# When stores are issued on a shared DMA queue: moving stores behind the operations that make them, and one kind of load to another queue

## The chip, the core and the metric

The kernel runs on one core of a Trainium2 chip. The core has engines that each run their own list of instructions in order: TensorE (PE in the profile; its weight loads are PEld), VectorE (DVE), ScalarE (ACT), GpSimd (POOL) and SyncE (SP), which here only issues DMAs. A DMA is issued from the list of one of these engines, and if the data that it reads or the buffer that it writes isn't ready, the engine's list stands at that instruction until it is. The metric is the time of the kernel on the device in microseconds (us).

## What is computed

The input `x` has the shape (4, 1024, 256), in float32. Two layers follow each other, both with a residual:

```python
x = x + attn(layernorm(x), w_attn, w_proj)
x = x + ffn(layernorm(x), ...)
```

`attn` is causal self-attention with 16 heads of 16 values over the 1024 positions of each of the 4 sequences, with a bias that falls off with distance by a slope for each head:

```python
att = einsum('bhqd,bhkd->bhqk', q, k) / sqrt(D) + where(rel <= 0, slopes * rel, -inf)
y = einsum('bhqk,bhkd->bhqd', softmax(att), v)
return y.transpose(0, 2, 1, 3).reshape(B, T, C) @ w_proj.T
```

`ffn` first attends over the 4 sequences at each position, which is a small attention of 4 by 4 for each position and head, then normalises, and then chooses an expert: each row of 256 values goes through one of 8 two-layer networks with a GELU, the one with the larger number among its two best. Its output is added and normalised again:

```python
h = layernorm(x + attn_out)
_, top_i = top_k(softmax(h @ router_w.T + router_b), 2)
assign = max(top_i, axis=-1)                  # one expert for each row
out[row] = gelu(h[row] @ w1[e].T + b1[e]) @ w2[e].T + b2[e]   # e = assign[row]
return layernorm(h + out)
```

## The kernel before, in words

The work is one long program in `fast_layer`, with the order of the instructions fixed by the kernel itself: the framework adds the semaphores, and doesn't reorder.

**Attention.** The rows are cut into 16 batches `n`, each of 256 positions (`W`) of one sequence: `batches[n] = (c, b)`, where `c` is the block of positions and `b` the sequence, with `c` running outside. The attention of a batch is a unit `u`; for the last block (`c` = 3) each batch is two units of 128 positions, so there are 20 units. The 16 heads are taken in 4 groups `g` of four. In a unit, each group takes one to three *rounds* of scores; a round is PE's `score` (line 955: 16 small products `sk` or more, two `exp` on ACT that write `p`, and a mask on POOL, line 986), and later PE's `weigh` (line 992), which multiplies the probabilities `p` with the values `v` into `pv`.

Two rounds are a *place* `p` of the main loop (lines 2242 to 2254); there are 80 places. Each place has two times at which other work is put between the scores: `E_slot(2p)` and `E_slot(2p + 1)`, half places, for elementwise work and for DMAs that are due, and `D_slot(p)` for products on PE. What goes where comes from two tables, `of_E` and `of_D`, filled at lines 2104 to 2120, from lists of work with due times, `due_E` and `due_D` (line 2129), and from a planner that keeps its own estimate of the time on PE, DVE and ACT (`time`) and starts the steps of the second layer when their inputs should be there.

**What goes through DRAM.** Three things are written to DRAM by one unit and read by others.

- *Keys and queries.* `project_qk` (line 879) makes half of the heads' queries and keys, copies them from PSUM to `kq` on DVE and stores them to `k_of[b]` (line 895 for `c` = 0, line 899 after). `fill_slots` (line 925) loads the keys of all positions so far and the queries, laid out with 32 rows for each head, into `slots` (line 939): four DMAs for each group and unit, issued when the unit before has done its last round of that group.
- *Values.* `value` (line 901) makes a batch's values, copied by ACT into `values[b % 2]`, and stores them to `v_of[b]` (line 916). `load_values` (line 918) loads the values of all earlier blocks of the sequence into `values[b % 2]` (line 923), since the two buffers are shared by the four sequences. It is put at `E_slot(2q + 1)`, where place `q` is the first of the unit before.
- *Outputs.* After a group pair's last round, `weigh` stores `yt` to `y_of[u]` (line 1036). Row 16 of each head's 32 holds the sum of its probabilities. `load_sums` (line 1043) reads the sums back (line 1045), `invert` (line 1049) takes the reciprocal on DVE and stores it to `r_of[u]` (line 1053), `load_y` (line 1057) loads the reciprocals spread over 16 rows into `su` (line 1068) and the outputs into `yc` (line 1071), `divide` multiplies the two on DVE, and `project` multiplies with `w_proj` on PE and adds to `x`. In the planner's time these steps are due 7, 14, 18, 29 and 31 us after the unit's last `weigh` (line 76).

For `c` = 0 the stores of `y` and `v` are issued by ACT. All other DMAs named here are issued by SP, in the order of the program.

**The second layer.** `front` (line 1551) is a generator with a step for each piece of work on one block of 128 positions of all four sequences: it normalises into `u`, projects, attends over the sequences, adds, normalises again and picks the expert. Two DMAs store the rows for the experts: `x` plus a bias, in four parts (line 1569, from `for_later`), and `u` (line 1768). Most fronts run inside the attention; at most two at a time (`start_fronts`). The buffers of `x` are ten; `load_next` loads a later batch's `x` when `left_x` says that both fronts of an earlier block have stored theirs. The last front and the experts, which gather their rows with indirect DMAs on POOL (line 1813) and scatter the results (line 1929), come after the attention, in the loops from line 2356 on.

Of the kernel before, what the change touches and what calls it, by code (L numbers as in the profile page):

```python
# [47 lines left out]
PC = W // P  # L48
# [557 lines left out]
def fast_layer(ctx: ExitStack, tc: tile.TileContext, odd, x, wq, wk, wv, wp, w_in, w_out, w_r,  # L606
# [244 lines left out]
    wqk = const("wqk", [P, 2, CC, C], into=pad)  # L851
    held = {}

    def x_norm(n, stage):
        c, b = batches[n]
        src = lambda i: xs[c, b][:, i]
        if stage == 0:
            held["norm", n] = norm_stats(src, PC, f"x_{n}", "_x")
        elif stage == 1:
            norm_root(held["norm", n][1], PC)  # L860
        else:
            xn = act.tile([P, PC, C], F32, tag="xn", name=f"xn_{n}")
            norm_apply(lambda i: xn[:, i], src, PC, *held.pop(("norm", n)), f"x_{n}")
            held["xn", n] = xn
# [14 lines left out]
    def project_qk(n, half):  # L879

        c, b = batches[n]
        xt = held["xt", n]
        pm = bank(f"qkp_{n}_{half}")
        for k in range(2):
            for cc in range(CC):
                nc.tensor.matmul(
                    pm[:, k * W:(k + 1) * W], wqk[:, k, cc, half * P:(half + 1) * P],
                    xt[:, cc], start=cc == 0, stop=cc == CC - 1,
                )
        kq = act.tile([P, 2, W], F32, tag=f"kq{half}", name=f"kq_{n}_{half}", bufs=KQ_BUFS)  # L890
        nc.vector.tensor_copy(kq.rearrange("p k w -> p (k w)"), pm)
        rows_ = slice(half * P, (half + 1) * P)
        if c == 0:
            held["kq", n, half] = kq
            nc.sync.dma_start(k_of[b][rows_, :2 * W], kq.rearrange("p k w -> p (k w)"))
        else:
            own = k_of[b][rows_, :W]
            both = bass.AP(own.tensor, own.offset, [own.ap[0], ((c + 1) * W, 2), (1, W)])
            nc.sync.dma_start(both, kq)

    def value(n):
        c, b = batches[n]
        xt, vt = held.pop(("xt", n)), values[b % 2]
        pm = bank(f"vp_{n}")
        for i in range(PC):
            for cc in range(CC):
                nc.tensor.matmul(
                    pm[:, i * C:(i + 1) * C], xt[:, cc, i * P:(i + 1) * P], wv_sb[:, cc],
                    start=cc == 0, stop=cc == CC - 1,
                )  # L910
        own = vt[:, PC * c:PC * (c + 1)]
        nc.scalar.copy(
            own[:, :, 0:H * VD].rearrange("p n (h d) -> p n h d", d=VD)[:, :, :, 0:D],
            pm.rearrange("p (n h d) -> p n h d", n=PC, d=D),
        )
        (nc.sync if c else nc.scalar).dma_start(v_of[b][:, PC * c:PC * (c + 1)], own)

    def load_values(u):
        n, i, _ = units[u]
        c, b = batches[n]  # L920
        known = NT if i else PC * c
        if known:
            nc.sync.dma_start(values[b % 2][:, :known], v_of[b][:, :known])

    def fill_slots(u, g):

        n, i, _ = units[u]
        c, b = batches[n]
        if b == 0 and c and i == 0:
            query_rows(c, g)  # L930
        for j in range(4):
            at, row_ = slice(j * S, j * S + D), (4 * g + j) * D
            n_cols = W + (c + 1) * W
            src = k_of[b][row_:row_ + D, :n_cols]
            if c == 0:
                row_ = (4 * (g % 2) + j) * D
                src = held["kq", n, g // 2][row_:row_ + D].rearrange("p k w -> p (k w)")
            queue = nc.scalar if u == 0 and j % 2 else nc.sync
            queue.dma_start(slots[g][at, :n_cols], src)
# [52 lines left out]
    def weigh(rounds_):  # L992
# [29 lines left out]
        for k, ((u, g), of_part) in enumerate(parts):  # L1022
            n, i, size = units[u]
            c = batches[n][0]
            pv = pm[:, k * W:k * W + size * P]
            if of_part[0][0] == 0 and g % 2 == 0:
                held["yt", g // 2] = ends.tile(
                    [P, 2, W], F32, tag="yt", name=f"yt_{u}_{g}", bufs=2
                )
            yt = held["yt", g // 2][:, :, :size * P]  # L1030
            if of_part[0][0] == 0:
                nc.scalar.copy(yt[:, g % 2], pv)
            else:
                nc.vector.tensor_tensor(yt[:, g % 2], yt[:, g % 2], pv, ALU.add)
            if g % 2 and of_part[-1][0] == n_rounds(u) - 1:
                (nc.sync if c else nc.scalar).dma_start(
                    y_of[u][g - 1:g + 1].rearrange("g p w -> p g w"), yt
                )

    def heads_of(n):  # L1040
        return y_of[n].rearrange("g p w -> (g p) w").rearrange("(h s) w -> h s w", s=S)

    def load_sums(u):
        part_of_row = units[u][2] * H
        nc.sync.dma_start(
            sums[u], heads_of(u)[:, D].rearrange("h (k w) -> h k w", w=part_of_row)
        )
# [503 lines left out]
    def front(i, fact, more, last):  # L1551
# [14 lines left out]
        def for_later(t):  # L1566

            nc.vector.tensor_tensor(at_x(t), at_x(t), row(B2), ALU.add)
            nc.sync.dma_start(rows_of[:, t, C:2 * C], at_x(t))

        def flipped(src, name):
            dst = fact.tile(
# [16 lines left out]
        yield "E", 1.7  # L1589
        for t in range(B):  # L1590
            for_later(t)
        left_x[i // PC] += 1
        yield "DQ" if more else "D", 2.8
        qkv = fact.tile([P, B, 3 * C + E], F32, tag="qkv", name=f"qkv_{i}")

# [169 lines left out]
        yield "E", 2.2  # L1765
        nc.vector.tensor_tensor(u, u, wide(row(G1)), ALU.mult)
        nc.vector.tensor_tensor(u, u, wide(row(B1)), ALU.add)
        nc.sync.dma_start(rows_of[:, :, 0:C], u)
        yield ("DC" if last else "D"), 0.8

        if last:
# [270 lines left out]
        return end  # L2042

    def start_fronts():
        while queue and len(running) < 2:
            running.append(Running(queue.pop(0)))

# [56 lines left out]
    for u, (n, i, size) in enumerate(units):  # L2104
        c, b = batches[n]

        q = begins[u - 1] if u else -2
        e = begins[u + 1]
        if u == n:
            if n > 2:  # L2110
                at_E(2 * begins[n - 3], lambda n=n: to_load.append(n))
            for k in range(3):
                at_E(2 * q - 7 + k, lambda n=n, k=k: x_norm(n, k), (1.0, 0.0, 0.8)[k])
            at_D(q - 2, 0.9, lambda n=n: turn(n))

            at_D(q - (n == 0), 1.7, lambda n=n: project_qk(n, 0))
            at_D(q + (n > 0), 1.7, lambda n=n: project_qk(n, 1))
            at_D(q + 2, 1.7, lambda n=n: value(n))
        if u > 1:
            at_E(2 * q + 1, lambda u=u: load_values(u))  # L2120


    due_E, due_D = [], []
# [67 lines left out]
    def E_slot(k, some=True):  # L2191
        for cost, what in of_E.pop(k, []) + pop_due(due_E, time["PE"]):
            what()
            busy("DVE", cost)
        load_next()
        if tables and fetching:
            experts.fetch()
# [44 lines left out]
    for p in range(len(rounds) // 2):  # L2242
# [10 lines left out]
        fill()  # L2253
        E_slot(2 * p + 1, then)
    weigh_next(waiting)
    attention.close()
    half_of.clear()
    tail_banks.append(ctx.enter_context(pool("ps_m", 3, space=PSUM)))
# [72 lines left out]
    def take(it, at):  # L2331
# [4 lines left out]
        for cost in it.more:  # L2336
            free["PE"] = max(free["PE"], at) + cost
        it.next()
        it.ready = end + LAG
        if on == "PE" and it.kind != "d":  # L2340
            it.ready = end + COPIED
# [34 lines left out]
    n = 0  # L2376
# [98 lines left out]
```

## Time and profile before

| | |
|---|---|
| median of 3 runs | 839.2 us |
| lowest, highest | 836.48, 842.09 us |
| the profiled execution | 839.28 us, its span 837.1 us |
| mean clock granted to PE | 0.940 |

The span runs from the first to the last instruction, and some 2 us lie around it. All durations below come from this one execution. Lines of the profile name an engine, the line of the kernel, an operation and what it writes and reads (`out<-in`). Nearly all instructions of PE, DVE and ACT are recorded through one helper at line 587, so they are told apart by what they write; DMAs have their own line. `SPq` is SP's list, in which a DMA's time is that of its issue and not of the transfer. The page's last part counts the DMAs, with the size of each:

```profile
slots<-k SPq DMA_DIRECT2D x128, 80.0 KB
k<-kq SPq DMA_DIRECT2D x32, 256.0 KB
v<-v SPq DMA_DIRECT2D x16, 288.0 KB
v<-v SPq DMA_DIRECT2D x4, 1152.0 KB
x<-in_x_dram SPq DMA_DIRECT2D x16, 256.0 KB
y<-yt SPq DMA_DIRECT2D x16, 256.0 KB
rows<-x SPq DMA_DIRECT2D x32, 128.0 KB
slots<-k SPq DMA_DIRECT2D x64, 64.0 KB
rows<-u SPq DMA_DIRECT2D x8, 512.0 KB
```

The 16 `v` DMAs of 288 KB are 12 stores and 4 loads; the loads of later blocks have 576, 864 and 1152 KB, four each. SP's list carries 79.63 MB on its queue (q1), ACT's 4.25 MB (q10).

### The profile page before, as it was taken

The page shows a single profiled execution, that of the slowest core. Times are in us where ns is not written, and L with a number is a line of the kernel's source. Part 1 is how long each engine was busy: PE and PEld are TensorE (multiplying, and loading weights), DVE is VectorE, ACT ScalarE, POOL GpSimd, SP SyncE. Part 2 cuts the span into 40 slices and gives each one's busy share as a digit, 9 for nine tenths or more (in the row PEclk, how much of TensorE's full clock was granted, in tenths as well). Part 3 has the DMA queues.
Part 4 walks back from the last instruction along what each step waited for, and adds up shares of the span by engine and source line. Part 5 has one row for each costly group of instructions (what it writes and reads, how often), then busy time and mean ns, then how long its engine had stood idle before and what let it go on. Part 6 is the DMA issues. An engine that isn't in the chain of part 4 may idle for free. (4 is left out here: it accounts for less than half of the span.)

```text
span 837.1 us, 22503 instructions
## 1 busy us (share of the span) xinstructions
PE 719.4 (86%) x8917; PEld 540.2 (65%) x8917; DVE 544.6 (65%) x1316; ACT 416.6 (50%) x625; POOL 251.1 (30%) x360
## 2 busy tenths in 40 slices
PE   4988879995999999998989999999983689678982
PEld 2766657674666756665667767787762368567772
DVE  7337224546678877946964739487695869884663
ACT  1455436563647556735654658578460235323540
POOL 5534102211113221102211212122130235637885
PEclk9799889998999999998999999999997699978997
DMA  7454444424344324333354635445315512333430
GB/s 215 117 148 137 143 134 134 144 63 123 94 119 129 108 77 147 98 104 95 93 142 141 185 109 144 123 126 158 94 53 195 177 37 90 93 97 120 124 103 24
DMA packets 75219, 99.56 MB, mean 119 GB/s; under 512 B 19496, under 2 KB 58723, under 8 KB 74596
## 3 DMA queue, kind: packets, MB, share of 16 engines
q1 hardware_dynamic: 64576, 79.63, 32.1%
q0 software_dynamic: 4864, 14.16, 5.6%
q10 hardware_dynamic: 5668, 4.25, 1.7%
q8 instruction: 73, 1.20, 0.6%
q14 instruction: 38, 0.31, 0.1%
HBM read 61.55 MB, written 35.12 MB: 115 GB/s over the span
## 5 line engine op out<-in xcount | busy, mean ns | idle before, releaser
L587 ACT ACTIVATE p<-sk 128x1024 f32<-128x1024 f32 (+1 forms) x320 | 287.0, 939 | 162.8 <-PE sk L587 147.8
L986 POOL TENSOR_SCALAR_AFFINE_SELECT p<-p 128x512 f32<-128x512 f32 (+1 forms) x160 | 103.6, 651 | 397.8 <-ACT p L587 395.9
L587 PE MATMUL sk<-slots 32*128 32x128 f32 (+1 forms) x3456 | 181.7, 328 | 21.2 <-DVE kq L587 10.0
L587 PEld LDWEIGHTS sk<-slots 32*128 32x128 f32 x3456 | 138.1, 188 | 64.9 <-issue 26.8
L587 PE MATMUL pv<-p,v 128*32 128x128 f32 (+1 forms) x3456 | 144.5, 314 | 10.4 <-ACT p L587 4.6
L587 PEld LDWEIGHTS pv<-p,v 128*32 128x32 f32 x3456 | 96.7, 111 | 48.3 <-issue 8.3
L587 PE MATMUL qkvp<-w_in,ut 128*128 128x264 f32 (+1 forms) x224 | 79.1, 489 | 0.0
L587 PEld LDWEIGHTS qkvp<-w_in,ut 128*128 128x128 f32 x224 | 40.3, 194 | 26.7 <-issue 22.4
L587 PE MATMUL oe<-w,ge 128*128 (+1 forms) x152 | 45.2, 423 | 12.9 <-DVE given L587 4.5
L587 PE MATMUL qkp<-xt,wqk 128*128 128x256 f32 x208 | 54.4, 407 | 0.2 <-ACT p L587 0.2
L1813 POOL DMA_INDIRECT given<-rows,rows x38 | 43.2, 1137 | 27.6 <-DVE at_t L587 11.6
L587 PE MATMUL hid<-mt,w 128*128 128x128 f32 x304 | 47.0, 293 | 0.5 <-ACT ge L587 0.5
L587 PEld LDWEIGHTS qkp<-xt,wqk 128*128 128x128 f32 x208 | 39.6, 200 | 11.1 <-issue 3.3
L587 ACT COPY qkv<-qkvp 128x512 f32<-128x512 f32 (+1 forms) x28 | 15.3, 555 | 58.5 <-PE qkvp L587 43.9
L587 PEld LDWEIGHTS hid<-mt,w 128*128 128x128 f32 x304 | 41.9, 200 | 2.0 <-ACT ge L587 1.0
L587 DVE COPY qkv<-qkvp 128x264 f32<-128x264 f32 x28 | 11.9, 431 | 46.9 <-PE qkvp L587 46.8
L1929 POOL DMA_INDIRECT out_dram<-o,out_rows x38 | 38.9, 1024 | 8.8 <-issue 6.3
L587 DVE TENSOR_REDUCE sc<-pr 128x64 f32<-128x1024 f32 x32 | 39.0, 1220 | 1.1
L587 PEld LDWEIGHTS oe<-w,ge 128*128 128x128 f32 x152 | 28.0, 205 | 17.8 <-DVE given L587 5.7
L587 DVE TENSOR_TENSOR pv<-qkv,sc 128x1024 f32<-128x1024 f32 x32 | 39.2, 1224 | 0.4 <-issue 0.3
L587 DVE TENSOR_TENSOR pr<-qkv 128x1024 f32<-128x1024 f32 x32 | 39.2, 1226 | 0.0
L587 PE MATMUL vp<-wv,xt 128*128 128x256 f32 x128 | 35.3, 423 | 0.0
(333 smaller groups left out, 1040.2 us busy)
## 6 DMA issues: line engine op xcount, KB each, us to landing
slots<-k SPq DMA_DIRECT2D x128, 80.0 KB
k<-kq SPq DMA_DIRECT2D x32, 256.0 KB
v<-v SPq DMA_DIRECT2D x16, 288.0 KB
v<-v SPq DMA_DIRECT2D x4, 1152.0 KB
x<-in_x_dram SPq DMA_DIRECT2D x16, 256.0 KB
y<-yt SPq DMA_DIRECT2D x16, 256.0 KB
rows<-x SPq DMA_DIRECT2D x32, 128.0 KB
slots<-k SPq DMA_DIRECT2D x64, 64.0 KB
```

What stands on the lines that cost most here:

```text
L587: ins = made(*args, **kwargs)
L986: nc.gpsimd.affine_select(blocks, blocks, pattern=[[0, 2], [0, size], [1, P]], compare_op=ALU.is_ge, fill=0.0, base=0, channel_multiplier=-1,)
L1813: nc.gpsimd.indirect_dma_start(out=self.hx, out_offset=None, in_=t.rows_of, in_offset=bass.IndirectOffsetOnAxis(ap=t.rows_[:, self.j:self. ...
L1929: ins = nc.gpsimd.indirect_dma_start(out=out.rearrange("t n c -> (t n) c"), out_offset=bass.IndirectOffsetOnAxis(ap=t.table.out_rows[:, t. ...
```

## The change

A list `stores` takes the place of issuing at once: a store is put on it with a key and an age, and is issued at the next `E_slot` that finds it with an age of one, or just before a load that reads what it writes. The stores of `k` and `v` for `c` > 0, of `y` for `c` > 0, and of `x` and `u` go this way. The age is raised at each `E_slot`, after the stores of age one have gone and before the front's steps of that slot, so that a store from a `weigh` goes half a place later, one from a `D_slot` between half a place and a place, and one from a front's elementwise step a whole place later. `start_fronts` issues waiting stores of `u` before it starts a front. In the loop after the attention, all stores on the list go right after the step that made them.

`load_values` is issued from ACT's list and not from SP's, and half a place later. The first half of `project_qk` comes one place earlier for `c` > 0. The stores of `x` of one front go together, after all four additions, and `left_x` is raised when they are issued.

```diff
@@ -851,6 +851,19 @@
     wqk = const("wqk", [P, 2, CC, C], into=pad)
     held = {}
 
+
+
+    stores = []
+
+    def store(key, what):
+        stores.append([key, 0, what])
+
+    def issue_stores(*keys, age=None):
+        due = [it for it in stores if it[0] in keys or age is not None and it[1] >= age]
+        for it in due:
+            stores.remove(it)
+            it[2]()
+
     def x_norm(n, stage):
         c, b = batches[n]
         src = lambda i: xs[c, b][:, i]
@@ -896,7 +909,7 @@
         else:
             own = k_of[b][rows_, :W]
             both = bass.AP(own.tensor, own.offset, [own.ap[0], ((c + 1) * W, 2), (1, W)])
-            nc.sync.dma_start(both, kq)
+            store(("k", n, half), lambda: nc.sync.dma_start(both, kq))
 
     def value(n):
         c, b = batches[n]
@@ -913,14 +926,19 @@
             own[:, :, 0:H * VD].rearrange("p n (h d) -> p n h d", d=VD)[:, :, :, 0:D],
             pm.rearrange("p (n h d) -> p n h d", n=PC, d=D),
         )
-        (nc.sync if c else nc.scalar).dma_start(v_of[b][:, PC * c:PC * (c + 1)], own)
+        to = v_of[b][:, PC * c:PC * (c + 1)]
+        if c:
+            store(("v", b), lambda: nc.sync.dma_start(to, own))
+        else:
+            nc.scalar.dma_start(to, own)
 
     def load_values(u):
         n, i, _ = units[u]
         c, b = batches[n]
         known = NT if i else PC * c
         if known:
-            nc.sync.dma_start(values[b % 2][:, :known], v_of[b][:, :known])
+            issue_stores(("v", b))
+            nc.scalar.dma_start(values[b % 2][:, :known], v_of[b][:, :known])
 
     def fill_slots(u, g):
 
@@ -931,6 +949,7 @@
         for j in range(4):
             at, row_ = slice(j * S, j * S + D), (4 * g + j) * D
             n_cols = W + (c + 1) * W
+            issue_stores(("k", n, g // 2))
             src = k_of[b][row_:row_ + D, :n_cols]
             if c == 0:
                 row_ = (4 * (g % 2) + j) * D
@@ -1033,15 +1052,18 @@
             else:
                 nc.vector.tensor_tensor(yt[:, g % 2], yt[:, g % 2], pv, ALU.add)
             if g % 2 and of_part[-1][0] == n_rounds(u) - 1:
-                (nc.sync if c else nc.scalar).dma_start(
-                    y_of[u][g - 1:g + 1].rearrange("g p w -> p g w"), yt
-                )
+                to = y_of[u][g - 1:g + 1].rearrange("g p w -> p g w")
+                if c:
+                    store(("y", u), lambda to=to, yt=yt: nc.sync.dma_start(to, yt))
+                else:
+                    nc.scalar.dma_start(to, yt)
 
     def heads_of(n):
         return y_of[n].rearrange("g p w -> (g p) w").rearrange("(h s) w -> h s w", s=S)
 
     def load_sums(u):
         part_of_row = units[u][2] * H
+        issue_stores(("y", u))
         nc.sync.dma_start(
             sums[u], heads_of(u)[:, D].rearrange("h (k w) -> h k w", w=part_of_row)
         )
@@ -1566,7 +1588,11 @@
         def for_later(t):
 
             nc.vector.tensor_tensor(at_x(t), at_x(t), row(B2), ALU.add)
-            nc.sync.dma_start(rows_of[:, t, C:2 * C], at_x(t))
+
+        def store_later():
+            for t in range(B):
+                nc.sync.dma_start(rows_of[:, t, C:2 * C], at_x(t))
+            left_x[i // PC] += 1
 
         def flipped(src, name):
             dst = fact.tile(
@@ -1589,7 +1615,7 @@
         yield "E", 1.7
         for t in range(B):
             for_later(t)
-        left_x[i // PC] += 1
+        store(("x", i), store_later)
         yield "DQ" if more else "D", 2.8
         qkv = fact.tile([P, B, 3 * C + E], F32, tag="qkv", name=f"qkv_{i}")
 
@@ -1765,7 +1791,7 @@
         yield "E", 2.2
         nc.vector.tensor_tensor(u, u, wide(row(G1)), ALU.mult)
         nc.vector.tensor_tensor(u, u, wide(row(B1)), ALU.add)
-        nc.sync.dma_start(rows_of[:, :, 0:C], u)
+        store(("u", i), lambda: nc.sync.dma_start(rows_of[:, :, 0:C], u))
         yield ("DC" if last else "D"), 0.8
 
         if last:
@@ -2042,6 +2068,8 @@
         return end
 
     def start_fronts():
+        if queue and len(running) < 2:
+            issue_stores(*[it[0] for it in stores if it[0][0] == "u"])
         while queue and len(running) < 2:
             running.append(Running(queue.pop(0)))
 
@@ -2113,11 +2141,11 @@
                 at_E(2 * q - 7 + k, lambda n=n, k=k: x_norm(n, k), (1.0, 0.0, 0.8)[k])
             at_D(q - 2, 0.9, lambda n=n: turn(n))
 
-            at_D(q - (n == 0), 1.7, lambda n=n: project_qk(n, 0))
+            at_D(q - (n == 0 or c > 0), 1.7, lambda n=n: project_qk(n, 0))
             at_D(q + (n > 0), 1.7, lambda n=n: project_qk(n, 1))
             at_D(q + 2, 1.7, lambda n=n: value(n))
         if u > 1:
-            at_E(2 * q + 1, lambda u=u: load_values(u))
+            at_E(2 * q + 2, lambda u=u: load_values(u))
 
 
     due_E, due_D = [], []
@@ -2192,6 +2220,9 @@
         for cost, what in of_E.pop(k, []) + pop_due(due_E, time["PE"]):
             what()
             busy("DVE", cost)
+        issue_stores(age=1)
+        for it in stores:
+            it[1] += 1
         load_next()
         if tables and fetching:
             experts.fetch()
@@ -2253,6 +2284,7 @@
         fill()
         E_slot(2 * p + 1, then)
     weigh_next(waiting)
+    issue_stores(age=0)
     attention.close()
     half_of.clear()
     tail_banks.append(ctx.enter_context(pool("ps_m", 3, space=PSUM)))
@@ -2336,6 +2368,7 @@
         for cost in it.more:
             free["PE"] = max(free["PE"], at) + cost
         it.next()
+        issue_stores(age=0)
         it.ready = end + LAG
         if on == "PE" and it.kind != "d":
             it.ready = end + COPIED
```

## The prediction

> **What bounds the kernel now.** I read the engines' busy shares first, then the table of stretches, then who waited for whom, and last the order of time around the largest hole.
>
> ```profile
> PE 719.4 (86%) x8917; PEld 540.2 (65%) x8917; DVE 544.6 (65%) x1316; ACT 416.6 (50%) x625; POOL 251.1 (30%) x360
> ```
>
> TensorE (PE) is the fullest engine. In the stretches of 20 us its busy time shows where it isn't full. The columns are PE, PEld, DVE, ACT and POOL busy, the granted clock, the DMA share and GB/s:
>
> ```profile
> 80.00:100.00 20.00, 16.06 (x113) 12.08 (x114) 6.90 (x20) 7.16 (x10) 2.11 (x4) 0.83 0.44 124
> 100.00:120.00 20.00, 14.77 (x145) 11.14 (x147) 3.88 (x13) 5.68 (x8) 1.28 (x2) 0.83 0.51 144
> ...
> 180.00:200.00 20.00, 11.23 (x184) 7.65 (x176) 11.27 (x13) 9.32 (x13) 3.85 (x6) 0.92 0.23 61
> ...
> 380.00:400.00 20.00, 16.75 (x203) 9.94 (x202) 16.55 (x41) 10.72 (x14) 3.28 (x5) 0.83 0.39 114
> ...
> 420.00:440.00 20.00, 16.21 (x336) 13.55 (x339) 11.43 (x20) 11.52 (x17) 3.56 (x6) 0.91 0.48 140
> ```
>
> Over 40 to 620 us, the attention, PE stands idle 41.7 us (20 minus its busy time, summed over 29 stretches). These five hold 25.0 of it. In them VectorE (DVE) is not full either: it stands too. The waits over the whole span (total, times, longest) say for what:
>
> ```profile
> DVE inverse L587 <- DMA sums<-y: 40.9, 8, 11.0
> ...
> DVE yc L587 <- DMA yc<-y: 28.2, 7, 8.6
> ...
> PE sk L587 <- DVE kq L587: 10.0, 3, 8.5
> ...
> PE op L587 <- DVE yc L587: 5.8, 1, 5.8
> ```
>
> So DVE stands 69.1 us for transfers, and PE then for DVE. Both transfers are issued by SyncE's queue (SP). Its own waits between 40 and 640 us:
>
> ```profile
> SPq L1036 <- ACT yt L587: 72.2, 20, 8.3
> ...
> SPq L1068 <- DMA r<-inverse: 22.9, 10, 5.3
> ...
> SPq L916 <- ACT v L587: 19.3, 8, 5.0
> SPq L899 <- DVE kq L587: 18.9, 7, 5.0
> ...
> SPq L939 <- DMA k<-kq: 14.6, 7, 3.0
> ```
>
> SP stands mostly in front of stores whose data isn't made yet. With the rows for other releasers: y stores (L1036) 100.4, k stores (L899) 28.0, v stores (L916) 19.3, u stores (L1768) 14.2, x stores (L1569) 9.0 us, 171 in all, and 14.6 for k to land before slots are read back. The worst hole in order of time:
>
> ```profile
> 182.81 0.38 SPq L1036 DMA_DIRECT2D y<-yt  x1
> 182.88 0.34 DVE L587 RECIPROCAL inverse<-sums 128x32 f32<-128x32 f32 x1
> ...
> 183.28 1.80 SPq L939 DMA_DIRECT2D slots<-k  x4
> ...
> 185.18 0.37 SPq L1053 DMA_DIRECT2D r<-inverse  x1
> ...
> 194.15 0.69 DVE L587 TENSOR_TENSOR yc<-yc,su 128x512 f32<-128x512 f32 x1 [8.59 <-DMA yc<-y]
> ...
> 200.27 2.19 PE L587 MATMUL sk<-slots 32*128 32x256 f32 x16 [8.53 <-DVE kq L587]
> ```
>
> The y store held SP until 182.81; the inverse, ready at 183.2, was stored at 185.18 only, behind four slot loads; DVE stood until 194.15, and PE until 200.27 for the kq copy queued behind. From about 640 us on, fronts and experts end in a chain on POOL (L1813, L1929).
>
> **What the Trainium skill says.** "DMA: Bandwidth & Descriptors", Anatomy of one DMA, says that a DMA's semaphore wait is served on the issuing sequencer before dispatch, and that most of a fixed cost of about 2 us is the receipt of the written bytes. The trace agrees: L1036 stands on SP, and r, issued at 185.18, lets su go at 186.84. Its Queues, rings and completion order gives SP and ACT a ring each on the same 16 DMA engines, served in turn; so a large load on ACT's ring lets a small one on SP's pass, where on one ring it goes ahead. No run yet shows that gain. "TensorE: Matmul & The Clock Gate", HAM oscillation, says that idle gaps over about 3.4 us throttle PE. It fits: the 16 score matmuls after the 8.53 us gap took 2.19 us, against 0.94 to 1.15 elsewhere, and the five stretches have clocks of 0.83 to 0.92.
>
> **The change part by part.** What is at stake: 25.0 us of holes and the 5.8 us at 630 us (op waiting for yc), 31 together. The lower clock in these stretches and the one after the third (0.91), one minus clock times PE busy, is 12 us more: 43 at most, 0.62 us for each of the 69.1 us that DVE stands.
>
> *y, k and v stores later.* No DMA is added; 32 y, 24 k and 12 v stores go to the next or next but one half place (about 4 us each: 80 places in some 600 us). By then the slot loads, which pace SP, have had their PE wait and the store's data is mostly there. What was queued behind a y store (3.1 us each, 100.4/32), above all slots, sums, r, su and yc, moves up. I go through the holes. At 82 to 92, SP stood about 3 us for k to land before eight slot loads; sums came last, at 88.55: half 0 of qk is now projected a place earlier, so I take 3 us off DVE's stall and 2 off PE's. At 102 to 113 sums was issued at 108.12 behind a v store, a 3 us wait for k and a 288 KB values load: 5 us off the 5.2 that PE stood and its start-up. At 185 to 194: r at 183.3 in place of 185.18, 2 us. At 391 to 397: r and yc earlier by one y wait, 1 us. At 426 to 432: sums came behind a y store and slot loads, 2 us. At 630: y stood 0.5 us between r and su: 0.5. Sum 12.5 us of 31; the same share of 12 is 5 us of clock. Bounds: 0 if all waits merely change name, 43 if all go.
>
> *What the delay adds.* A k store of half 1 is forced just before the slot load that needs it, where a group has two rounds (8 units): landing costs SP up to 3.0 us each, as the k row shows, 24 us of SP at most; the slots are needed four places later, so I take 1 us on PE. Queued behind are r, su and yc, and DVE waits for those. A y store forced by its sums would do likewise, but a unit's sums come 5.7 to 18 us behind its own last y store (276.02 to 281.68, 469.96 to 487.94): 0. Buffers: yt is written again two places on, u with the next but one front, x loads come after x stores (353.21, then 355.11) but have places to spare; 0 each, up to 4 us (a 512 KB u store before DVE may write) if that cover goes.
>
> *Values on ACT.* Sixteen loads of 288 to 1152 KB leave SP: 16 x 0.37 us of issue, and their bytes leave its ring. They cost ScalarE the same 6 us, where it is 50 to 65% busy between exps. Its wait, for PE's weighing of the unit before last, is over by then, since the exp ahead of it needs a later PE product. I take 1 us on PE; bounds 0 and 6, plus any wait. The gain by the ring isn't seen in this trace; 0 to 3 us for each of eight sums stalls, I take 1 us over all.
>
> *x and u stores, tail.* 32 and 8 stores; SP stood 23 us for them in the attention, and little hung on it: 1 us. In the tail stores go out at once after each step; the four x stores come after four adds instead of between. 0, within 1 us either way. The planner's slots shift with the moved projection; which front steps fit changes: plus or minus 5 us.
>
> Sum: 12.5 + 5 - 1 - 1 + 1 + 1 = 17.5 us off; I take off 3.5 for stalls that come back at the next wait, r's landing (22.9 us on SP, untouched): 14. The profiled execution took 839.28 us, its span 837.1; 825.3. The median, 839.2, is the same; I forecast **825 us**.
>
> **The rivals.** *First: new waits swallow it.* Every sums and yc still needs store, landing, load, landing, and DVE has as little between inverse and divide as before (two operations at 183). If DVE's stalls fall by only 5 of 69 us, 5 x 0.62 gives 836. For it: r's 22.9 us and the 3.4 to 5.2 us that sums take to land. Against: stores stand for 171 us. *Second, slower: stores now land in front of their own readers.* If a forced k or y store stands ahead of the sums chain in most of the 16 units past the first four, at 3.0 us each, DVE stands 48 us longer less the gain of 23 (14/0.62): 25 x 0.62 is 15 us, 855. It decides from where forced landings outlast the 23 us, eight of them. Against: the gaps of 5.7 us and more between y and its sums. A projection moved onto a busy place would add to it. *Third: the stores aren't later in fact.* Stores asked for by a reader at once keep the old order; then only the values move, 837.
>
> **How the numbers follow.** Forecast 0.62 (its own range 812 to 831), first and third rival together 0.24 (831 to 846), second 0.14 (846 to 862). 8 times in 10: 808, where 31 of the 43 us have gone, to 846, where part of the second's case is left out. One per cent, 8.4 us, is about what can be told from no change. Faster 0.62, same 0.24, slower 0.14.
>
> **What would show it.** Right: L1036 on SP falls under 40 us; DVE for sums and yc falls from 69 to about 45; PE fills 80 to 120 and 180 to 200, clock 0.95 or more. Values loads stand on ACT at 0.37 us with no wait. Wrong: SP's waits reappear as DMA k or y under L939 and L1045, DVE stands as long, or exps wait behind a values load. If the time goes after 640 us, the prediction missed the tail.

## The result, and the profile after

| | before | after |
|---|---|---|
| median of 4 runs each, same chip | 837.84 us | 826.3 us |
| lowest, highest | 836.25, 842.09 us | 822.12, 827.67 us |
| profiled execution, its span | 839.28, 837.1 us | 827.67, 825.9 us |
| mean clock granted to PE | 0.940 | 0.949 |

The ratio after to before is 0.9864, with a 95% interval of 0.983 to 0.9898: the change makes the kernel 1.4% faster. The profile of the changed kernel is read in the same order as that of before. Its busy time by engine first:

```profile
PE 708.6 (86%) x8917; PEld 532.4 (64%) x8917; DVE 544.8 (66%) x1316; ACT 416.5 (50%) x625; POOL 253.6 (31%) x360
```

The numbers of instructions are those of before. The span less PE's busy time is 117.3 us, against 117.7, so the gain of 11.2 us of span doesn't show as less idle time of PE: it is in PE's busy time (10.8 us less). A busy PE is not one at full speed: one minus the clock, times PE's busy time, is 43.2 us before and 36.1 after, so by this estimate about 7 us of the 10.8 are clock; what the rest is isn't shown.

The stretches that held the holes, after the change (columns as before: PE, PEld, DVE, ACT, POOL, clock, DMA share, GB/s):

```profile
80.00:100.00 20.00, 13.93 (x133) 10.35 (x136) 9.30 (x26) 9.41 (x15) 3.31 (x5) 0.83 0.48 139
100.00:120.00 20.00, 17.82 (x212) 13.27 (x200) 2.81 (x10) 10.40 (x15) 3.90 (x6) 1.00 0.40 121
120.00:140.00 20.00, 12.72 (x148) 8.90 (x148) 8.08 (x22) 7.01 (x9) 2.31 (x4) 0.83 0.40 118
...
180.00:200.00 20.00, 19.48 (x275) 13.70 (x277) 18.69 (x30) 13.53 (x20) 5.62 (x8) 1.00 0.56 158
...
380.00:400.00 20.00, 16.51 (x217) 11.20 (x215) 18.17 (x39) 11.05 (x14) 3.71 (x5) 0.91 0.41 115
...
420.00:440.00 20.00, 20.00 (x376) 16.73 (x369) 8.16 (x18) 11.80 (x17) 3.22 (x7) 1.00 0.71 177
```

The holes at 180 to 200 and at 420 to 440 are gone: 275 matmuls where there were 184 in the first, 376 for 336 in the second, and the full clock in both. The one at 380 to 400 is as it was (16.51 us of PE for 16.75). Those at 80 to 120 are not gone. The first is deeper (13.93 for 16.06), and the second has moved on to 120 to 140, where PE had been full before (20.00) and is now busy for 12.72 us at a clock of 0.83. The waits over the whole span (total, times, longest):

```profile
DVE inverse L587 <- DMA sums<-y: 30.7, 6, 14.6
...
DVE yc L587 <- DMA yc<-y: 19.2, 5, 6.7
...
PE sk L587 <- DVE passed L587: 8.3, 1, 8.3
```

DVE stands 49.9 us for the two transfers, where it stood 69.1. One wait for sums alone is 14.6 us, where the longest of before was 11.0, and the 8.3 us that PE stands in the last line comes from it. SP's own waits between 40 and 640 us:

```profile
SPq L958 <- PE sk L587: 78.6, 48, 7.2
SPq L958 <- DVE slots L587: 48.3, 8, 11.9
SPq L958 <- DMA k<-kq: 38.4, 16, 3.9
...
SPq L1057 <- DVE yt L587: 11.5, 2, 6.7
SPq L1067 <- DMA y<-yt: 9.5, 3, 4.5
```

Line 1036 is now 1057, 939 is 958, 1045 is 1067, 1068 is 1090. SP no longer stands at the y stores: with its other rows, L1057 has 27.9 us where it had 100.4. It stands at the slot loads, which come next in its list: the rows of L958 that wait for an engine and not for a DMA add up to 158 us, where they were 87. Nearly all of it is for PE and DVE, so the loads themselves couldn't have gone earlier; but whatever is behind them in SP's list waits too. Two rows are dearer than before: k's landing in front of slot loads, 38.4 us in 16 waits where it was 14.6 in 7, and y's landing in front of sums, 9.5 us, for which before has no row.

### The profile page after: what moved, and what is told of

Same layout as the page of the kernel before. It is cut to its first block, busy times and chain, and to the rows that moved or that the text cites. A ratio compares the mean times of both kernels' runs of the same rounds, so it can differ in the third digit from the quotient of the medians.

```text
span 825.9 us, 22497 instructions
## 1 busy us (share of the span) xinstructions
PE 708.6 (86%) x8917; PEld 532.4 (64%) x8917; DVE 544.8 (66%) x1316; ACT 416.5 (50%) x625; POOL 253.6 (31%) x360
## 5 line engine op out<-in xcount | busy, mean ns | idle before, releaser
L1005 POOL TENSOR_SCALAR_AFFINE_SELECT p<-p 128x512 f32<-128x512 f32 (+1 forms) x160 | 105.6, 664 | 396.6 <-ACT p L587 394.6
L587 PE MATMUL oe<-w,ge 128*128 (+1 forms) x152 | 43.4, 410 | 14.4 <-DVE given L587 6.0
L587 DVE COPY qkv<-qkvp 128x264 f32<-128x264 f32 x28 | 12.1, 432 | 54.1 <-PE qkvp L587 54.1
L587 PE MATMUL hid<-mt,w 128*128 128x128 f32 x304 | 47.2, 293 | 0.4 <-ACT ge L587 0.4
L587 ACT COPY qkv<-qkvp 128x512 f32<-128x512 f32 (+1 forms) x29 | 16.1, 557 | 59.0 <-PE qkvp L587 47.1
```

The lines of the kernel that those rows point to most:

```text
L587: ins = made(*args, **kwargs)
L1005: nc.gpsimd.affine_select(blocks, blocks, pattern=[[0, 2], [0, size], [1, P]], compare_op=ALU.is_ge, fill=0.0, base=0, channel_multiplier=-1,)
```

## The experiments

Units are counted from 0 in this text: unit 7 is the eighth, its first `exp` is at 187.4 us, and the largest hole of before, PE's stand until 200.27 us, lies in it. Each kernel was timed beside the kernel before on the same chip; ratios are to that. The changed kernel delays five kinds of store, moves the values' loads, and moves one product of PE by a place; the first four runs take these apart.

### One part of the change alone

**The stores.** The changed kernel, with values loaded by SP at their old time and the projection at its old place:

```diff
-            nc.scalar.dma_start(values[b % 2][:, :known], v_of[b][:, :known])
+            nc.sync.dma_start(values[b % 2][:, :known], v_of[b][:, :known])
...
-            at_D(q - (n == 0 or c > 0), 1.7, lambda n=n: project_qk(n, 0))
+            at_D(q - (n == 0), 1.7, lambda n=n: project_qk(n, 0))
...
-            at_E(2 * q + 2, lambda u=u: load_values(u))
+            at_E(2 * q + 1, lambda u=u: load_values(u))
```

> Only the stores are issued later; values and the first half of qk as before. Order of PE, DVE and POOL as before. Stores theory (SP stood in front of stores, so sums, r and yc came late): most of the 11.5 us, 827 to 832, ratio about 0.988 to 0.992, DVE's waits for sums and yc under 55 of 69 us. Order theory (the gain comes from the moved projection, which lays out PE's and DVE's work anew): 836 to 840, same. Values theory (the large loads leave SP's ring): 836 to 840, same.

Measured: 832.86 us, ratio 0.9946 (0.9923 to 0.9968). All of the stores' delay is worth 0.5%. That lies between what the two theories gave, and what it bought in the largest hole is shown further down.

**The moved projection.** The kernel before, with one call of the planner's table changed:

```diff
-            at_D(q - (n == 0), 1.7, lambda n=n: project_qk(n, 0))
+            at_D(q - (n == 0 or c > 0), 1.7, lambda n=n: project_qk(n, 0))
```

> Only the first half of qk is projected a place earlier for c > 0; all DMAs from the lists and at the moments of before. This alone gives PE, DVE and POOL the order that they have in the changed kernel. Order theory: most of the gain, 827 to 831, and the seventh unit takes about 31 us where it took 41. Stores theory: within 4 us of before, 834 to 842, and the seventh unit keeps its hole of 8.5 us.

Measured: 822.67 us, ratio 0.9829 (0.9805 to 0.9854). This one line, with every store still issued at once (a k store goes earlier only with its own projection), gives more than the other parts together and more than the order theory expected, and its median is below that of the whole change. SP still stands at the y stores as it did; the largest of their rows between 40 and 640 us:

```profile
SPq L1036 <- ACT yt L587: 67.6, 18, 8.3
```

With the other rows it is 99.5 us, against 100.4 before. SP's wait for y, which the prediction took for the root of the holes, is hardly changed, and the time has gone.

**The values.** The kernel before, with only the load moved:

```diff
-            nc.sync.dma_start(values[b % 2][:, :known], v_of[b][:, :known])
+            nc.scalar.dma_start(values[b % 2][:, :known], v_of[b][:, :known])
...
-            at_E(2 * q + 1, lambda u=u: load_values(u))
+            at_E(2 * q + 2, lambda u=u: load_values(u))
```

> Only the values' loads are issued by ACT, half a place later. Values theory: DVE's waits for sums shrink by 1 to 3 us each at 82 to 113 us, 832 to 836. Stores and order theory: 837 to 840, no change; ACT carries 16 issues of about 0.37 us.

Measured: 839.12 us, ratio 1.0022 (1.0005 to 1.0039): nothing, or a little lost.

**All but the projection.** The changed kernel with the projection back at its old place:

```diff
-            at_D(q - (n == 0 or c > 0), 1.7, lambda n=n: project_qk(n, 0))
+            at_D(q - (n == 0), 1.7, lambda n=n: project_qk(n, 0))
```

> The whole change without the moved projection; order of PE, DVE and POOL as before. Stores theory: 826 to 830, as the changed kernel. Order theory: 835 to 840, and the hole of the seventh unit is still there, since the copy of kq still stands behind the divide on DVE.

Measured: 832.01 us, ratio 0.9929 (0.9905 to 0.9952). So the DMA parts make 0.7% in the old order, and the moved projection on top of them another 0.7%, to 1.4%. The parts don't add up: the projection alone has 1.7%, so in the new order the DMA parts as a whole gain nothing and may lose a little (0.9864 against 0.9829; the intervals overlap).

What does one place of one product reach? With the lists of instructions laid beside each other, the three kernels with the old projection have exactly the order of before on PE, DVE and POOL, and the one with the moved projection alone has that of the changed kernel (on PE, four neighbouring records of 8917 stand in another order). The planner charges nothing for stores and loads; so of all the edits this one alone can re-lay the work of the engines that compute. And it re-lays more than itself: the later steps, with their due times, fall into other slots: 182 of the 1316 places in DVE's list hold another operation. The stretch between the reciprocal of unit 5 and the divide that needs its result, on DVE:

| kernel | DVE's operations between | their work | DVE's wait ahead of the divide |
|---|---|---|---|
| before | 2 | 2.4 us | 8.6 us |
| stores alone | 2 | 2.4 us | 5.5 us |
| after | 10 | 11.0 us | none |
| moved projection alone | 10 | 11.0 us | 2.6 us |

From the reciprocal through its store, the loads and their landing to the divide are 11.27 us before (182.88 to 194.15). With the stores alone they are 8.15: `r` goes out at 183.09, much as the prediction had it (183.3), and 3.1 us of DVE's 8.6 go. So lateness was part of it. What the order decides is what DVE does meanwhile. In the changed kernel, in order of time:

```profile
180.85 0.34 DVE L587 RECIPROCAL inverse<-sums 128x32 f32<-128x32 f32 x1
...
183.14 0.37 SPq L1075 DMA_DIRECT2D r<-inverse  x1
...
184.81 0.61 SPq L1090 DMA_DIRECT2D su<-r  x1
...
186.19 0.68 DVE L587 COPY kq<-qkp 128x512 f32<-128x512 f32 x1
...
186.74 0.57 SPq L1093 DMA_DIRECT2D yc<-y  x1
...
190.57 1.22 DVE L587 TENSOR_REDUCE sc<-pr 128x64 f32<-128x1024 f32 x1
191.71 0.68 DVE L587 TENSOR_TENSOR yc<-yc,su 128x512 f32<-128x512 f32 x1
```

From reciprocal to divide are 10.86 us. The last row has no idle time in front of it, so this is the time of DVE's own work, and says nothing of the transfers. The `kq` copy, for which PE stood 8.53 us before, now stands ahead of the divide in DVE's list (186.19), and the front's products and sums fill the rest. With the projection moved alone, the same order hides the chain although the stores are where they were:

```profile
176.59 0.34 DVE L587 RECIPROCAL inverse<-sums 128x32 f32<-128x32 f32 x1
...
181.64 0.37 SPq L1053 DMA_DIRECT2D r<-inverse  x1
181.93 0.68 DVE L587 COPY kq<-qkp 128x512 f32<-128x512 f32 x1
...
190.10 0.69 DVE L587 TENSOR_TENSOR yc<-yc,su 128x512 f32<-128x512 f32 x1 [2.57 <-DMA slots<-k]
```

Here `r` goes out 5.0 us after its reciprocal and the chain takes 13.5 us, longer than before, yet DVE stands 2.57 us instead of 8.59. (The profile puts this wait down to a slot load, which the divide doesn't read; the landings of `su` and `yc` fall into the same time.)

### One call moved, and the due times

If order at this one spot is the cause, then moving the projection of one unit only should give most of the gain, and so should putting the divide later in some other way. The two runs, both on the kernel before:

```diff
-            at_D(q - (n == 0), 1.7, lambda n=n: project_qk(n, 0))
+            at_D(q - (n == 0 or n == 7), 1.7, lambda n=n: project_qk(n, 0))
```

> The kernel before, with one call moved: the first half of qk of batch 7 alone is projected a place earlier. On DVE 19 operations, some 9 us of work, then stand between the reciprocal of unit 5 and its divide, where two stood. Order theory: the hole at 191 to 200 us closes, unit 7 takes 31 to 33 us in place of 40.9, and the time falls by 7 to 10 us, 827 to 830. Rival (the moved projection helps by earlier k stores, all over): 1 to 2 us of change, 835 to 838.

Measured: 822.95 us, ratio 0.9833 (0.9791 to 0.9874), as much as all twelve moved calls and more than was expected. The lists of DVE and PE differ from those of before only between 147 and 205 us. Between the reciprocal and the divide DVE now has 19 operations with 14.1 us of work:

```profile
180.25 0.34 DVE L587 RECIPROCAL inverse<-sums 128x32 f32<-128x32 f32 x1
...
182.93 0.38 SPq L1036 DMA_DIRECT2D y<-yt  x1
...
185.30 0.37 SPq L1053 DMA_DIRECT2D r<-inverse  x1
...
195.37 0.69 DVE L587 TENSOR_TENSOR yc<-yc,su 128x512 f32<-128x512 f32 x1 [1.22 <-DMA yc<-y]
```

The y store goes out at 182.93 and `r` at 185.30, to 0.12 us as in the kernel before (182.81 and 185.18). The very delay that the prediction charged for the hole is there, and the hole is not: DVE stands 1.22 us. The rival, that earlier k stores help all over, is out, since only one goes earlier here.

```diff
-SUMS_BY, INVERTED_BY, Y_BY, DIVIDED_BY, PROJECTED_BY = 7.0, 14.0, 18.0, 29.0, 31.0
+SUMS_BY, INVERTED_BY, Y_BY, DIVIDED_BY, PROJECTED_BY = 7.0, 14.0, 18.0, 35.0, 37.0
```

> The kernel before, with the divide due 35 and the projection due 37 in place of 29 and 31 in the planner's time; no DMA is moved in its own rules. At least 8 operations then stand between each reciprocal and its divide but for none. Order theory: DVE's wait for yc falls from 28 to under 8 us and PE loses the holes behind it, 820 to 830. Rival (SP's pace decides, and DVE then stands elsewhere): sums' wait grows by as much, 834 to 842.

Measured: 827.61 us, ratio 0.988 (0.9842 to 0.9918). With the divide due 6 us later, 18 operations (10.7 us) lie in that stretch, and the wait for `yc` is gone from the whole list. The expected rival came true as to the waits, though not as to the time: those for sums have grown to take its place.

```profile
DVE inverse L587 <- DMA sums<-y: 64.6, 10, 15.4
```

DVE stands 64.6 us for the two transfers, almost the 69.1 of before, and the kernel is 10 us faster. So the total of a wait over a span says little about its worth: laid against PE's own idle time, PE was idle for 12.9 us of DVE's 69.1 before, and for 6.4 of these.

Two things changed together in all the kernels that close this hole: DVE has more to do before the divide, and the `kq` copy, for which PE stands next, comes ahead of it. No run parts the two. But the second bears on the price: the divide of unit 6 in the changed kernel has 2 operations before it, and DVE stands 4.27 us (until 228.89), with PE idle for none of that time.

Where the gains lie shows in the progress of the profiled executions, by the first `exp` of a unit. The column of before has its time in us; the others give the difference to it:

| first exp of unit | before | after | projection alone | unit 7 alone | stores alone | after, k at once |
|---|---|---|---|---|---|---|
| 4 | 83.8 | +4.2 | +5.1 | +2.2 | +2.5 | +6.2 |
| 5 | 126.8 | +2.7 | -2.7 | +1.0 | +0.7 | -1.7 |
| 7 | 187.4 | +2.3 | -2.0 | +0.1 | -0.2 | -2.7 |
| 8 | 228.3 | -7.8 | -11.9 | -8.6 | -2.8 | -12.8 |
| 12 | 407.5 | -6.4 | -10.7 | -8.9 | -2.8 | -12.1 |
| 15 | 496.7 | -12.4 | -17.1 | -12.5 | -7.1 | -20.5 |
| 20 (last exp) | 624.4 | -10.4 | -16.7 | -12.1 | -6.6 | -21.1 |

Unit 7 gives about 10 us in the kernels with all projections moved (+2.3 to -7.8 after), 8.7 where only its own is, and 2.6 with the stores alone. The units 12 to 14 give 3.6 to 8.4 in all of them, the stores alone 4.3; the 3.6 are those of unit 7 alone, where the order there is that of before, so part of this follows from the earlier shift and isn't explained here. Up to unit 5 the changed kernel has lost 2.7 us, and the last column, which is the next run, shows to what.

### k stores at once, in the new order

The new wait of 14.6 us lies in unit 4. Around it, in the changed kernel:

```profile
117.10 0.46 SPq L912 DMA_DIRECT2D k<-kq  x1
...
121.49 1.71 SPq L958 DMA_DIRECT2D slots<-k  x4
...
123.25 0.56 SPq L1067 DMA_DIRECT2D sums<-y  x1
...
125.40 0.35 DVE L587 RECIPROCAL inverse<-sums 128x32 f32<-128x32 f32 x1 [14.57 <-DMA sums<-y]
...
127.28 2.19 PE L587 MATMUL sk<-slots 32*128 32x256 f32 x16 [8.26 <-DVE passed L587]
```

A k store that is still held back is forced out just in front of the slot load that reads it (117.10). The load then stands for the store's landing, 3.9 us, and the sums, which come behind the slots on SP, are loaded at 123.25. DVE waits for them, and PE for the copies behind the reciprocal. With the projection alone moved, sums went out 4.9 us earlier in the same stretch, and PE stood 3.46 us instead of 8.26:

```profile
118.31 0.56 SPq L1045 DMA_DIRECT2D sums<-y  x1
...
120.95 0.35 DVE L587 RECIPROCAL inverse<-sums 128x32 f32<-128x32 f32 x1 [9.77 <-DMA sums<-y]
...
122.84 1.24 PE L587 MATMUL sk<-slots 32*128 32x256 f32 x16 [3.46 <-DVE passed L587]
```

The run takes the changed kernel and issues these stores, and only these, at once:

```diff
-            store(("k", n, half), lambda: nc.sync.dma_start(both, kq))
+            nc.sync.dma_start(both, kq)
```

> The changed kernel, but the k stores for c > 0 are issued at once again. Forced-landing theory (in the changed kernel a k store goes out just before the slot loads that read it, SP stands 3 to 4.4 us for it to land, and sums behind it come late): the fifth unit (u = 4) falls from 41.4 to about 36 us, and the time from 826.3 to 818 to 822. If the values' loads or the y stores cost the changed kernel its time against the projection alone (822.7): no change, 825 to 828.

Measured: 817.98 us, ratio 0.9762 (0.9728 to 0.9797): faster than both kernels, with the lowest median of all. From its first exp to that of unit 5, unit 4 takes 35.0 us instead of 41.4. DVE's waits over the span:

```profile
DVE inverse L587 <- DMA sums<-y: 20.0, 5, 7.0
...
DVE yc L587 <- DMA yc<-y: 16.6, 7, 7.4
```

The longest is 7.4 us, and SP's wait for k to land is 5.2 us where it was 38.4. Against the projection alone (0.9829) the later y, v, x and u stores and the values on ACT together gain 0.7%, the intervals being apart: once k isn't delayed, the DMA parts do pay in the new order. The same edit in the old order, with values on SP (the kernel with the stores alone, its k stores put back):

> Order of PE, DVE and POOL as before, values on SP; y, v, x and u stores later, k stores at once. Against s_only (832.9), which also delays the k stores. Forced-landing theory: SP's wait for k to land falls from 52 us to about 15, and the time to 828 to 831. If delaying the k stores was of no weight in the old order: 832 to 834.

Measured: 832.63 us, ratio 0.9929 (0.9903 to 0.9955), which can't be told from the stores alone (0.9946). SP's wait for k to land fell less than expected, from 47.2 us with the stores alone to 30.0, but those 17 us bought no time that shows. The delay of k costs some 8 us in the new order, and nothing that shows in the old.

### Values on ACT, once more

Three kernels have the new order and differ in which queue loads the values and in the stores. Stores later, values on SP as before:

> Moved projection and later stores, values on SP as before. If the later stores cost what the changed kernel loses against the moved projection alone: 825 to 828. If the values on ACT cost it: 820 to 823, and in both cases the order of PE, DVE and POOL is that of the changed kernel.

Measured: 828.24 us, ratio 0.989 (0.9851 to 0.9928), against 0.9864 with values on ACT: intervals overlap. With the projection alone at 0.9829 this fits that it is the later stores that take time back, and not the values; the intervals just touch. The same with k stores at once:

> As k_at_once, but the values' loads stay on SP at their old half place. If the values on ACT are worth something once no k store is forced: 1 to 4 us slower than k_at_once, 819 to 822. If they are worth nothing: 817 to 819.

Measured: 820.12 us, ratio 0.9803 (0.9781 to 0.9826), against 0.9762 with values on ACT; intervals just overlap. So k's delay is a loss with values on either queue (0.989 to 0.9803 here), and the values' move gains 0.3 and 0.4% in these two pairs, neither clear of the noise. With all stores at their old times, moved projection and values on ACT:

> Moved projection and values on ACT, all stores at once. If the values on ACT pay in the new order by themselves: 818 to 821, 2 to 4 us under the projection alone (822.7). If they pay only where the stores are later too: 822 to 825.

Measured: 827.67 us, ratio 0.9883 (0.9857 to 0.9909), where the projection alone has 0.9829. It lies outside what either theory gave: here the move costs half a per cent, and the intervals are apart. ACT's exps did wait for DMAs; the largest such row between 40 and 640 us:

```profile
ACT p L587 <- DMA su<-r: 5.0, 1, 5.0
```

But this one lies at 80 us, and by the first exp of unit 15 the kernel still had 16.1 us on the one before (the projection alone 17.1). That falls to 12.0 by the last exp (the projection alone: 16.7), so the loss lies in the last units. Two stands of PE there, 1.77 us in front of `sk` at 496.96 and 2.03 us in front of `pv` at 548.90, have no releaser in the profile. The kernel with values alone moved has the same two, 1.84 and 2.13 us, and the projection alone has neither. Their 3.8 us are about what the kernel loses there against the projection alone (3.7); what PE stood for isn't shown, so the cause stays open.

### The divide later as well

The best version, with the divide due 3 us later and the projection with it:

```diff
-SUMS_BY, INVERTED_BY, Y_BY, DIVIDED_BY, PROJECTED_BY = 7.0, 14.0, 18.0, 29.0, 31.0
+SUMS_BY, INVERTED_BY, Y_BY, DIVIDED_BY, PROJECTED_BY = 7.0, 14.0, 18.0, 32.0, 34.0
```

> As k_at_once, with the divide due 32 and the projection due 34 in the planner's time. Order theory: the remaining waits of DVE for yc (16.6 us) go, 812 to 817. Rival (a later due time only moves work to where PE is full, as the longer sums waits of divide_later suggest): 817 to 823.

Measured: 819.27 us, ratio 0.9796 (0.9774 to 0.9818), against 0.9762: no gain, as the rival had it. DVE's waits for `yc` fell from 16.6 to 10.1 us and those for sums stayed (20.6 for 20.0). It fits that these waits held up little by then; why the time didn't fall with them isn't shown.

## Why the prediction was right, and where it was wrong

The time and the direction were right: 825 forecast, 826.3 measured, inside the forecast's own range. The mechanism that carried the forecast was wrong in its main term, and errors of both signs cancelled: the DMA parts, from which 14 us were forecast, gave 5.2 by themselves (837.23 less 832.01), and a term left at zero made up for it. That the sum came out right was luck.

**"The planner's slots shift with the moved projection; which front steps fit changes: plus or minus 5 us."** This is the step that failed. It was left as a bound, taken as zero, without a look at which steps would move. Alone it is worth 14.6 us (837.23 less 822.67), about three times the stores. The working for the hole at 185 to 194 had the evidence in hand: two operations on DVE between reciprocal and divide, and a `kq` copy queued behind. The first rival even took it that DVE would have "as little between inverse and divide as before"; it got 10 operations. The prediction read the lateness of the transfer as the cause. Without that lateness unit 7 gained 2.6 us (stores alone); with `r` as late as before and another order it gained 8.7 (unit 7 alone). Costing a moved product meant asking what stands between each producer and its consumer afterwards; the prediction asked this of DMAs only.

**"Sum 12.5 us of 31; the same share of 12 is 5 us of clock"**, for stores issued later. 17.5 us were credited here. With the stores alone it is 4.4 us (837.23 less 832.86), k's delay included, which cost nothing that shows in that order. By holes: "At 82 to 92" 2 us, for the projection in fact, and "at 102 to 113" 5 us were credited. By unit 5 the projection alone has gained 2.7 us, the stores alone have lost 0.7 and the changed kernel 2.7. For 185 to 194 2 us were credited to the stores, and they gave 2.6: that step was right. For 426 to 432 2 us were credited, and the stores alone give 4.3 over the units 12 to 14. SP's waits at y stores did fall to 27.9 us, below the 40 named as a sign of being right; that sign came true, but SP went on to stand at slot loads, and the time hardly followed.

**"... landing costs SP up to 3.0 us each ... I take 1 us on PE."** The mechanism was right and its size was off, in the new order: the k row went from 14.6 to 38.4 us on SP, as much as the 24 named as the most, and on the kernel's time it is about 8.5 us (0.9864 less 0.9762, of 837; 7.3 us by the pair with values on SP). The slots themselves weren't late; the sums behind them on SP were. The prediction had written that `r`, su and yc are queued behind, and then priced only the slots. It is the second rival, real in part, within a kernel that gained elsewhere. For y stores and their own sums 0 was taken, since sums come "5.7 to 18 us behind". That reading left out the last two units (606.46 to 611.42 and 630.38 to 633.46 us before, 5.0 and 3.1 us). In the changed kernel SP waits 9.5 us in 3 for y to land ahead of sums, at the units 7, 12 and 18, and what that cost the kernel wasn't tried by itself.

**"0.62 us for each of the 69.1 us that DVE stands"** isn't a rate. The forecast of "about 45" for DVE's waits nearly held (49.9), but the divide put 6 us later saved 10 us of time with 4.5 us less of them.

**Values on ACT: 1 us gained by the ring, 1 us lost on ACT.** Alone the move adds 0.2% to the time, and with the new order -0.4 to +0.5%, by what else is in the kernel. Sixteen issues of about 0.33 us stand on ACT, nearly as said, but "with no wait" was wrong:

```profile
81.73 0.34 ACTq L587 DMA_DIRECT2D v<-v  x1
...
82.17 1.51 ACT L587 ACTIVATE p<-sk 128x768 f32<-128x768 f32 x2 [5.83 <-DMA b_bf<-pieces]
```

ACT stood 5.83 us at one of them, and the exp came behind it. The separate ring that the Trainium skill describes ("DMA: Bandwidth & Descriptors", Queues, rings and completion order) may let small loads pass, but no run here shows a gain of its own from it: the kernel with the values alone moved is not faster, and where the move seems to gain, the intervals overlap.

**Clock.** The prediction leaned on the Trainium skill, "TensorE: Matmul & The Clock Gate", HAM oscillation, for idle gaps that lower PE's clock. The trace agrees again: after the new gap of 8.26 us the 16 score matmuls take 2.19 us and the stretch has 0.83, while the two filled stretches have 1.00; after the gap of 3.46 us with the projection alone they take 1.24. But "0.94 to 1.15 elsewhere" was misread. In the kernel before, at 81.73 us, the same matmuls take 2.38 us after a gap of 2.56:

```profile
81.73 2.38 PE L587 MATMUL sk<-slots 32*128 32x256 f32 x16 [2.56 <-DMA slots<-k]
```

And at 393.74 they take 2.09 with no gap noted. So the gap just ahead doesn't by itself tell how slow they are. The mean over the span reached 0.949; the stretches from 80 to 100 and 120 to 140 stayed at 0.83, where 0.95 was asked for at 80 to 120.

**x and u stores, buffers, tail: about 0.** Nothing in the runs speaks against it: at the last exp the changed kernel is 10.4 us ahead and at its end 11.2, so what comes after the attention made less than 1 us of it. The x and u stores weren't tried by themselves.

What stays open: why the values on ACT cost half a per cent with stores at once and not with stores later, whether DVE's fuller list or the earlier `kq` copy is what closed the hole, and how the 3.6 to 8.4 us of the units 12 to 14 divide between order and stores.

## What to carry to other kernels

Where an engine waits for a transfer that it has itself set off, count the operations between the one that starts the chain and the one that needs its end, as well as asking why the transfer is late: with 11 us of other work in between, DVE stood 2.6 us or not at all where it had stood 8.6. And look at what is queued behind the wait, since a stand of DVE on which PE didn't depend cost PE nothing. In a kernel whose order comes from a planner, an edit that moves one product re-lays much of what follows, and has to be priced by the new order, if need be by laying the lists of instructions side by side. A store may be put off only if its reader is far enough behind: price not only the reader that then waits for the landing, but everything behind it in the same queue.

## What the runs showed of the hardware

A DMA in ACT's list can stand for a transfer of SP with which it has nothing to do. In the instruction lists of these kernels the DMAs of SP and ACT share the same eight completion semaphores, and in the two cases shown ACT's list waited, ahead of its DMA, for an earlier DMA of SP on the same semaphore to land. So the values load above stood for `b_bf<-pieces`, and in the kernel with projection and values moved an exp waited behind a y store of ACT for `su<-r`:

```profile
79.64 0.37 ACTq L587 DMA_DIRECT2D y<-yt  x1
80.11 1.51 ACT L587 ACTIVATE p<-sk 128x768 f32<-128x768 f32 x2 [4.96 <-DMA su<-r]
```

The engine stood 4.96 us for a small load on another queue that neither instruction reads. And a store of 256 KB that is read back at once took 4.39 us from its issue at 117.10 to the issue of the load that waits for it at 121.49, 3.9 us of it the wait for the landing. In this one case that is how far ahead of its reader the store should have been.
